# A state-space layer followed by windowed attention: order of the first loads, place of the attention's first loads and of the last statistics

## The chip, the cores and the metric

The kernel runs on one core of one Trainium2 chip. The metric is the device time of one execution in microseconds (us). Before the change it is 6751.26 us, the median of three runs (6746.82 to 6751.3). The profile comes from one more execution, which took 6765.22 us; its first and last instruction are 6763.5 us apart (its span). About 0.2%, or 13.5 us, is what a measurement of this kernel can tell from no change.

## The reference

Input x has shape (4, 384, 64, 64): four batches, 384 channels, 4096 positions each, float32. Two layers follow each other, both with a group normalisation in front and a residual behind:

```
x = x + ssm(gn(x))      # layer norm over channels, in_proj 384 -> 2*768, conv of 4 taps, silu,
                        # x_proj to dt (24), B (16), C (16), softplus, then per position
                        #   h = exp(dt*A)*h + dt*x*B ;  y = sum_n h*C     (16 states per channel)
                        # y + D*x, times silu(z), out_proj 768 -> 384
x = x + attn(gn(x))     # q, k, v = 1x1 conv; 12 heads of 32 channels; each position attends to the
                        # 7x7 window around it (edge padded) with a relative bias; softmax; 1x1 conv
```

The group normalisation takes mean and variance over 32 groups of 12 channels and all 4096 positions of a batch. So the second layer of a batch can't begin before the first layer of that batch has ended.

## The kernel before, in words

**Two layers, written out by hand.** `state_space_layer` works through 44 chunks of 372 or 376 positions, eleven per batch. Each part of a chunk (a load, a matrix product, a scan, a store) is put into a list with a tick; the list is sorted by tick and each engine gets its instructions in that order. `Written` (its `call` is line 152, which is why nearly every row of the profile says L152) ties each instruction of an engine to the one before it, so an engine never takes a later one first. This holds for SP too: SP issues all DMAs of the kernel, in the written order, and one that has to wait holds up all behind it. There are eight completion semaphores for DMAs, used in turn, so that a DMA also waits until the one issued eight before it has landed.

**The start.** Ahead of chunk 0, in a pool `fold` (lines 360 to 426): load `w_in`, `lnw`, `lnb`; load all of batch 0 into `xall` in eight pieces; load `cvb`, `dtb`, `dsk`, `w_cv`, `nega`, `xpw` and six pieces of `w_dt`; multiply `w_in` by `lnb` (PE) for `binp`, scale it by `lnw` (DVE); take the statistics of `xall` (24 `bn_stats`), and turn them into scale and shift `gm` by `stats_phases` (line 256: eight small steps that go PE, DVE, PE, DVE and POOL, PE, ACT, PE, DVE and POOL); store the scaled `w_in` to `wdr` in twelve pieces; build `dcv`, 24 diagonal matrices 128x128 from the identity and `w_cv`, on DVE, and store them to `ddr` in six pieces (lines 420 to 426). Line 469 then loads `qkb` and `pjb`. The first entry of the sorted list is `load_x` of chunk 0 (line 494, tick -732), which loads the tile `xn`; `gn` on ACT normalises it with `gm`, and the layer norm, `in_proj`, `conv` and so on follow.

**The end of the first layer.** Behind the last scan come the last `out_proj`, `residual` (line 799: DVE adds, SP stores to `x1`), and `out_stats` (line 807: `bn_stats` and `bn_aggr` on DVE), for three blocks of channels; then the eight steps of `stats_phases` for the last batch. Values, keys and queries of the second layer for batches 0 to 2 have by then been computed beside the scans and stored to `vdr`, `kdr`, `qdr`.

**The second layer.** `attention_layer` (line 1118) works through 32 stripes of 512 positions with twelve units each, and a loop variable `s` that counts units and starts three stripes early. Its tiles are in pools that open when those of the first layer close, so that the first instruction that writes such a tile waits for the last user of the memory below it. Ahead of unit 0, SP loads `bias` (two pieces, line 1447), `q` and `kt` for stripe 0, the same for stripe 1 (`load_keys`, line 1207), `w_pj`, and the values `vw` of the first pairs (`load_v`, line 1395). `surround` (line 1221) copies edges of `kt` on POOL. A unit has `scores` (PE products into `lg`, DVE adds the bias into `sg` and takes the maximum, ACT exponentiates), `divide` (DVE reciprocal, POOL multiply), `turn` (PE transposes, DVE and ACT copy) one to two units later, and `weigh` (PE) three later. At `s == 4` stands `output_bias`, 18 small products on PE.

Of the kernel before, what the change touches and what calls it, by code (L numbers as in the profile page):

```python
# [25 lines left out]
KC = 4  # L26
# [142 lines left out]
def two_layers(  # L169
# [151 lines left out]
    def store_values(dq, b, k, v):  # L321

        for row in range(2):
# [7 lines left out]
            for t in to:  # L331
                dq.dma_start(vdr[b][t, PAD : PAD + HW, :], v[a : a + HW, :])
                for c, p in ((0, a), (PAD + HW, a + HW - 1)):
# [2 lines left out]
                        v[p : p + 1, :].unsqueeze(1).broadcast_to([1, PAD, C]),  # L336
                    )

    def state_space_layer(eng):
        te, ve, se, ge, _ = eng  # L340
        gm1 = [const.tile([P, NJ, 3], F32, name=f"gm1_{b}") for b in range(NB)]
# [3 lines left out]
        with ExitStack() as es:  # L345
            def pool(name, **kw):
                return es.enter_context(tc.tile_pool(name=name, **kw))
# [13 lines left out]
            with tc.tile_pool(name="fold", bufs=1, side="right") as fold, tc.tile_pool(  # L361
                name="ps_fold", bufs=1, space=PSUM
            ) as fps:
                w_in = load([P, NJ, 2 * DI], in_wT.rearrange("(k p) m -> p k m", p=P), "w_in", fold)
                lnw, lnb = columns((ln_w, NJ, "lnw"), (ln_b, NJ, "lnb"))
                xall = fold.tile([P, NJ, L], F32, name="xall")
                xsrc = x[0].rearrange("(k p) t -> p k t", p=P)
                for k in range(NXT):
                    dq.dma_start(
                        xall[:, :, k * TX : (k + 1) * TX], xsrc[:, :, k * TX : (k + 1) * TX]  # L370
                    )
                cvb, dtb, dsk = columns(
                    (conv_b, ND, "cvb"), (dt_b, ND, "dtb"), (d_skip, ND, "dsk")
                )
                w_cv = load([P, ND, KC], conv_w.rearrange("(k p) m -> p k m", p=P), "w_cv", wt)
                nega = load([P, ND, NS], a_log.rearrange("(k p) n -> p k n", p=P), "nega", wt)
                xpw = load([P, ND, NX], xp_wT.rearrange("(k p) m -> p k m", p=P), "xpw", fold)
                for k in range(3):
                    for half in range(2):
                        d = 3 * half + k  # L380
                        dq.dma_start(
                            w_dt[32 * k : 32 * k + DTR, half * P : (half + 1) * P],
                            dt_wT[:, d * P : (d + 1) * P],
                        )

                se.preload_act_table_set("natural_log_exp_and_others")
                se.activation(nega, nega, AF.Exp)
                se.activation(nega, nega, AF.Copy, scale=-1.0)

                ge.memset(w_xp, 0.0)  # L390
                for k in range(3):
                    ge.tensor_copy(w_xp[:, :, 32 * k : 32 * k + DTR], xpw[:, :, :DTR])
                ge.tensor_copy(w_xp[:, :, 96:], xpw[:, :, DTR:])
                pb0 = fps.tile([P, 512], F32, name="pb0")
                for m in range(2 * ND):
                    for j in range(NJ):
                        te.matmul(
                            pb0[:, m : m + 1], w_in[:, j, m * P : (m + 1) * P], lnb[:, j : j + 1],
                            start=(j == 0), stop=(j == NJ - 1),
                        )  # L400
# [12 lines left out]
                gm0 = small.tile([P, NJ, 3], F32, tag="gm", name="gm_0")  # L413
                for phase in stats_phases(
                    (te, ve, se.activation, ge, lambda t: None), mv0, gm0, lambda: pb0, "a0"
                ):
                    phase()
                for m in range(2 * ND):
                    dq.dma_start(wdr[m], w_in[:, :, m * P : (m + 1) * P])
                dcv = fold.tile([P, ND, KC, P], F32, name="dcv")  # L420
                for d in range(ND):
                    for k in range(KC):
                        ve.tensor_scalar(
                            dcv[:, d, k, :], ident, w_cv[:, d, k : k + 1], None, ALU.mult
                        )
                    dq.dma_start(ddr[d], dcv[:, d, :, :])

            ps_a = pool("ps_a", bufs=1, space=PSUM, reuse_waits="tile")
            ps_x = pool("ps_x", bufs=1, space=PSUM, reuse_waits="tile")
            ps_y = pool("ps_y", bufs=1, space=PSUM, reuse_waits="tile")  # L430
            ps_m = pool("ps_m", bufs=1, space=PSUM, reuse_waits="tile")
            sb = pool("sb", bufs=1, reuse_waits="tile")

            free, kind_of = {}, {}

            def tile_of(shape, tag, bufs, home=sb):

                if tag not in free:
                    free[tag] = [
                        home.tile(shape, F32, name=f"{tag}{k}") for k in range(bufs)  # L440
                    ]
                    for t in free[tag]:
                        kind_of[id(t)] = tag
                return free[tag].pop(0)
# [20 lines left out]

            def put(tick, fn, *args):
                score.append((tick, len(score), fn, args))

            qkb, pjb = columns((qkv_b, 3 * NJ, "qkb"), (proj_b, NJ, "pjb"))


            def x_stats(b, j, i):
# [566 lines left out]
            for b in range(1, NB):  # L1039
# [9 lines left out]
                    put(tick - 3 * STEP, begin)  # L1049
                    put(tick, lambda cell=cell: cell.pop()())  # L1050
                in_phases(T0 - 3 * CHUNK + AT["x_norm"][0], AT["x_norm"][1:], lambda b=b: x_norm(b))
            for b in range(NB):
                in_phases(
                    CHUNK * NCHUNK * (b + 1) + AT["out_norm"][0], AT["out_norm"][1:],
                    lambda b=b: stats_phases(
# [45 lines left out]
                            put(CHUNK * X + AT[name][NJ * i + m], fn, cell, m)  # L1101


            put(-120, dq.dma_start, w_out, out_wT.rearrange("(k p) m -> p k m", p=P))
            put(-120, dq.dma_start, w_v, qkv_wT[:, 2 * C :].rearrange("(k p) m -> p k m", p=P))
            put(-100, lambda: se.activation(qs, qkb[:, 0:NJ], AF.Copy, scale=HD**-0.5))
# [7 lines left out]

            for _, _, fn, args in sorted(score, key=lambda e: e[:2]):
                fn(*args)
        return gm1, qkb, pjb
    def attention_layer(eng, gm1, qkb, pjb):
        te, ve, se, ge, dq = eng
        scale = HD**-0.5  # L1120
        stripes = NB * NXT
        with ExitStack() as es:
# [3 lines left out]
            wt = pool("wt1", bufs=1)  # L1126
            w_qkv = wt.tile([P, NJ, 3 * C], F32, name="w_qkv")
            pjv = wt.tile([P, NJ], F32, name="pjv")
            bias = wt.tile([P, NH, NK], F32, name="bias")
            w_pj = wt.tile([P, NJ, C], F32, name="w_pj")  # L1130

            psum = pool("psum1", bufs=1, space=PSUM)
# [8 lines left out]
            def ring(shape, tag, bufs, k):  # L1141

                if tag not in rings:
                    rings[tag] = [sb.tile(shape, F32, name=f"{tag}{i}") for i in range(bufs)]
                return rings[tag][k % bufs]

            def of(s):
# [57 lines left out]
                surround(s, m)  # L1205

            def load_keys(s):
                b, r = of(s)
                dq.dma_start(
                    q_of(s),  # L1210
                    qdr[b][:, r * TX : (r + 1) * TX].rearrange("(k p) t -> p k t", p=P),
                )
                for m in range(NJ):
                    dq.dma_start(
                        kt_of(s)[:, m, PAD : PAD + RB, PAD : PAD + HW],
                        kdr[b][m * P : (m + 1) * P, r * TX : (r + 1) * TX].rearrange(
                            "p (r c) -> p r c", r=RB
                        ),
                    )

            def surround(s, m):

# [169 lines left out]
                    ov[:, : NJ * P].rearrange("p (m q) -> p m q", m=NJ),  # L1392
                )

            def load_v(k):
                s, p = k // NPAIR, k % NPAIR
                b, r = of(s)
                vw = vw_of(k)
                for e in range(2):
                    for c in range(NCH):  # L1400
                        y, x0 = RB * r + c * RW // NCH, (2 * p + e) * CB
                        dq.dma_start(
                            vw[:KN, e, c, :],
                            vdr[b][y : y + RW // NCH, x0 : x0 + CW, :],
                        )


            N = stripes * UNITS
            waiting = []
            for s in range(-3 * UNITS, N + 12):  # L1410
                stripe, k = s // UNITS, s % UNITS
                for f in waiting:
# [1 line left out]
                waiting = []  # L1414
                if s == 4:
                    output_bias(mm)
                if 0 <= s - 4 < N and (s - 4) % NJ == NJ - 1:
                    keep(s - 4)
                if 0 <= s - 1 < N:
# [24 lines left out]
                        surround(stripe + 2, (k - 4) // 2)  # L1444
                if k == 2 and 0 <= stripe + 3 < stripes and not has_keys(stripe + 3):
                    load_x(stripe + 3)
                if s == 2 - 3 * UNITS:
                    for e in range(2):
                        dq.dma_start(
                            bias[e * QB : (e + 1) * QB].rearrange("p h k -> p (h k)"), bm  # L1450
                        )
                if s == 3 - UNITS:
                    dq.dma_start(w_pj, proj_wT.rearrange("(k p) m -> p k m", p=P))
                if s == 2 * UNITS:
# [2 lines left out]
                    gn(stripe + 3, k - 6)  # L1457
                pair = (s + 1) // NJ + 1
                if (s + 1) % NJ == 0 and 0 <= pair < stripes * NPAIR:
                    load_v(pair)  # L1460

    engines = [
        Written(tc, e) for e in (nc.tensor, nc.vector, nc.scalar, nc.gpsimd, nc.sync)
# [49 lines left out]
```

## Time and profile before

| | us |
|---|---|
| median of three runs | 6751.26 |
| profiled execution | 6765.22 |
| its span | 6763.5 |
| PE, DVE, ACT, POOL busy | 6286.7, 5867.9, 5708.1, 5668.5 |
| last matrix product of the first layer ends | 5246.7 |
| first score of the second layer on DVE | 5271.30 |

An engine's busy time is the sum over its instructions; four engines are busy for 84 to 93% of the span, and waits are spread over both layers. A time line row has the start in us, the duration in us, engine, line, operation and tiles, a count xN where equal ones were merged, and in brackets the idle time before it and what ended it. SPq rows are DMA issues: their duration is that of the issue on SP's queue, not of the transfer. A row of the chain of waits has a start, a duration and what the chain ran through; "issue" is time in which the engine waited for nothing that the profile shows.

### The profile page before, as it was taken

To read this page: it belongs to the slowest core of one execution; us is meant where nothing else is said; L and a number is where in the kernel's file an instruction comes from. 1 tells how busy PE (TensorE), PEld (TensorE's weight loads), DVE (VectorE), ACT (ScalarE), POOL (GpSimd) and SP (SyncE) were. 2 spreads that over 40 slices of the span, in tenths; PEclk is the share of its full clock that TensorE was granted. 3 is DMA by queue.
4 is the path that set the end of the run, shared out by engine and by line. 5 is a ranking of instruction groups with operands and counts; after the bars stand their busy time and mean duration, and the time that the engine had idled before them with its cause. 6 is when DMAs were issued, how large, how long until landed. Compare 5 with 4: busy or idle time off the path is not lost.

```text
span 6763.5 us, 135265 instructions
## 1 busy us (share of the span) xinstructions
PE 6286.7 (93%) x47526; PEld 4326.7 (64%) x47526; DVE 5867.9 (87%) x10258; ACT 5708.1 (84%) x14235; POOL 5668.5 (84%) x2788
## 2 busy tenths in 40 slices
PE   6888888988999999999999999999997899999999
PEld 4666666666667676666666666767665555555555
DVE  3999999999999999999999999999998566555555
ACT  3888888888999999999999999999996687665556
POOL 1999999999999999999999999999999555443443
PEclk9999999999999999999999999999998899999999
DMA  5242423233454535354444434453532555323332
GB/s 179 83 136 87 138 86 118 91 116 115 135 159 127 160 117 166 119 158 133 153 140 131 153 121 151 123 160 117 160 113 67 169 156 152 103 95 104 102 102 91
DMA packets 790241, 860.11 MB, mean 127 GB/s; under 512 B 200345, under 2 KB 710073, under 8 KB 789433
## 3 DMA queue, kind: packets, MB, share of 16 engines
q1 hardware_dynamic: 789560, 851.45, 40.7%
q8 instruction: 377, 6.18, 0.4%
q14 instruction: 304, 2.48, 0.1%
HBM read 740.60 MB, written 110.81 MB: 126 GB/s over the span
## 4 chain that ended last, share of the span: by engine, by line
PE 43%; ACT 21%; DVE 20%; issue 6%; POOL 6%; DMA 3%; SPq 1%; POOLq 0%; DVEq 0%; ACTq 0%
PE mm L152 28%; DVE h L152 17%; PE yps L152 7%; ACT da L152 6%; POOL h L152 6%; PE pt L152 4%; ACT L152 4%; ACT sg L152 3%; PE ov L152 2%; PE lg L152 2%; DMA w_in<-wdr 2%; ACT dt L152 1%; ACT sz L152 1%; ACT xb L152 1%; ACT pT L152 1%
## 5 line engine op out<-in xcount | busy, mean ns | idle before, releaser
L152 DVE TENSOR_TENSOR_SCAN h<-da,h 128x373 f32<-128x373 f32 (+1 forms) x4224 | 3658.6, 914 | 124.8 <-ACT da L152 109.7
L152 POOL TENSOR_TENSOR h<-h,BC 128x1488 f32<-128x1488 f32 (+1 forms) x1056 | 3255.9, 3100 | 116.6 <-ACT state L152 110.7
L152 ACT ACTIVATE da<-dt,nega 128x372 f32<-128x372 f32 (+1 forms) x4224 | 2361.7, 569 | 212.0 <-DVE h L152 194.3
L152 POOL TENSOR_TENSOR h<-dtx,BC 128x372 f32<-128x372 f32 (+5 forms) x836 | 1757.9, 2113 | 51.7 <-ACT dtx L152 41.2
L152 PE MATMUL yps<-ident,h 128*124 128x128 f32 (+1 forms) x12672 | 1587.2, 279 | 104.8 <-POOL h L152 104.5
L152 PEld LDWEIGHTS yps<-ident,h 128*124 128x124 f32 (+1 forms) x12672 | 1453.5, 142 | 261.2 <-POOL h L152 165.8
L152 PE MATMUL mm<-xn,w_in 128*128 128x372 f32 (+3 forms) x3168 | 1146.5, 503 | 102.4 <-DMA w_in<-wdr 47.7
L152 POOL TENSOR_TENSOR sg<-sg,rs 128x784 f32<-128x784 f32 x384 | 573.4, 1493 | 635.5 <-DVE rs L152 507.4
L152 ACT ACTIVATE sg<-sg,mx 128x196 f32<-128x196 f32 x1536 | 685.3, 448 | 389.8 <-DVE mx L152 381.2
L152 DVE TENSOR_TENSOR h<-dtxps,BC 128x1488 f32<-128x1488 f32 (+5 forms) x924 | 964.5, 1059 | 6.5 <-ACT dtx L152 4.6
L152 PEld LDWEIGHTS mm<-xn,w_in 128*128 128x128 f32 x3168 | 603.7, 200 | 470.5 <-issue 49.5
L152 PE MATMUL mm<-xb,cw 128*128 128x372 f32 (+1 forms) x2112 | 697.8, 476 | 7.1 <-DMA cw<-ddr 5.1
L152 ACT ACT_TABLE_LOAD x529 | 678.7, 1283 | 10.1 <-PEq L1498 0.8
L152 DVE CUSTOM_DVE_ANT_0 sg<-lg,bias 128x196 f32<-128x196 f32 x1536 | 464.4, 358 | 196.7 <-PE lg L152 195.6
L152 PE MATMUL mm<-yg,w_out 128*128 128x372 f32 (+1 forms) x1584 | 529.5, 480 | 22.0 <-DVE yg L152 21.9
L152 PEld LDWEIGHTS mm<-xb,cw 128*128 128x128 f32 x2112 | 389.8, 189 | 239.2 <-DVE h L152 6.0
L152 PE MATMUL pt<-ident,sg 128*98 128x128 f32 x3072 | 447.6, 281 | 29.5 <-ACT pT L152 21.3
L152 PEld LDWEIGHTS pt<-ident,sg 128*98 128x98 f32 x3072 | 314.4, 128 | 182.4 <-issue 81.6
L152 PEld LDWEIGHTS mm<-yg,w_out 128*128 128x128 f32 x1584 | 290.0, 190 | 183.7 <-DVE yg L152 30.3
L152 PEld LDWEIGHTS ov<-pT,vw 98*32 98x32 f32 x12288 | 189.8, 110 | 195.5 <-issue 139.5
L152 PE MATMUL mm<-xk,wk 128*128 128x256 f32 x1080 | 268.3, 390 | 46.2 <-ACT dt L152 46.2
L152 ACT ACTIVATION_READ_ACCUMULATOR sg<-sg,mx 128x1 f32 x1536 | 288.2, 188 | 0.0
(136 smaller groups left out, 7158.9 us busy)
## 6 DMA issues: line engine op xcount, KB each, us to landing
BC<-bcrows SPq DMA_DIRECT2D x320, 744.0 KB
w_in<-wdr SPq DMA_DIRECT2D x528, 192.0 KB
vw<-vdr SPq DMA_DIRECT2D x512, 147.0 KB
cw<-ddr SPq DMA_DIRECT2D x264, 256.0 KB
xs<-in_x_dram SPq DMA_DIRECT2D x210, 186.0 KB
wk<-in_qkv_wT_dram SPq DMA_DIRECT2D x180, 192.0 KB
o<-x SPq DMA_DIRECT2D x96, 256.0 KB
out_dram<-o SPq DMA_DIRECT2D x96, 256.0 KB
```

Source lines behind the costliest of these rows:

```text
L152: ins = made(*args, **kw)
```

## The change

The arithmetic stays the same. Three things are moved.

At the start, `w_cv` is loaded ahead of `xall`; `qkb` and `pjb` are loaded with the other small vectors; `dcv` is built on POOL instead of DVE, and its six stores stand ahead of the statistics and of the twelve stores of `wdr`:

```diff
                 lnw, lnb = columns((ln_w, NJ, "lnw"), (ln_b, NJ, "lnb"))
+                w_cv = load([P, ND, KC], conv_w.rearrange("(k p) m -> p k m", p=P), "w_cv", wt)
                 xall = fold.tile([P, NJ, L], F32, name="xall")
...
+                cvb, dtb, dsk, qkb, pjb = columns(
+                    (conv_b, ND, "cvb"), (dt_b, ND, "dtb"), (d_skip, ND, "dsk"),
+                    (qkv_b, 3 * NJ, "qkb"), (proj_b, NJ, "pjb"),
+                )
...
+                dcv = fold.tile([P, ND, KC, P], F32, name="dcv")
+                for d in range(ND):
+                    for k in range(KC):
+                        ge.tensor_scalar(
+                            dcv[:, d, k, :], ident, w_cv[:, d, k : k + 1], None, ALU.mult
+                        )
+                    dq.dma_start(ddr[d], dcv[:, d, :, :])
                 se.preload_act_table_set("natural_log_exp_and_others")
...
                 for m in range(2 * ND):
                     dq.dma_start(wdr[m], w_in[:, :, m * P : (m + 1) * P])
-                dcv = fold.tile([P, ND, KC, P], F32, name="dcv")
-                for d in range(ND):
-                    for k in range(KC):
-                        ve.tensor_scalar(
-                            dcv[:, d, k, :], ident, w_cv[:, d, k : k + 1], None, ALU.mult
-                        )
-                    dq.dma_start(ddr[d], dcv[:, d, :, :])
```

At the end of the first layer, the tiles that are not needed by its last instructions (`xn`, `sq`, `w_in`, `xb`, `cw`, `xd`, `xk`, `yk`, `wk`, `xv`, `vo`) now have a pool `prep` of their own on the right side of the memory. It closes behind the last of their users, and in its place opens a pool `early` with `kt` for stripes 0 and 1, `q` for stripe 0, `vw` for pair 0 and `bias`. Their loads are put at a tick behind the first `residual` of the last chunk and ahead of its second (605), so in SP's order the stores of the second and third `residual` stand behind them. `load_keys` and `load_v` leave out what is there:

```diff
+            def begin_attention():
+                preps.close()
+                home = ctx.enter_context(
+                    tc.tile_pool(name="early", bufs=1, reuse_waits="tile", side="right")
+                )
...
+                for s in range(2):
+                    load_stripe_keys(dq, kt[s], s)
+                load_stripe_queries(dq, q, 0)
+                load_pair_values(dq, vw, 0)
+                for e in range(2):
+                    dq.dma_start(bias[e * QB : (e + 1) * QB].rearrange("p h k -> p (h k)"), bm)
+
+            put(
+                CHUNK * (len(chunks) - 1) + 1 + max(
+                    max(AT[name]) for name in ("key_store", "value_store", "in_bias", "conv")
+                ),
+                begin_attention,
+            )
...
             def load_keys(s):
...
+                if s > 0:
+                    load_stripe_queries(dq, q_of(s), s)
+                if s > 1:
+                    load_stripe_keys(dq, kt_of(s), s)
...
                 if (s + 1) % NJ == 0 and 0 <= pair < stripes * NPAIR:
-                    load_v(pair)
+                    if pair > 0:
+                        load_pair_values(dq, vw_of(pair), pair)
```

The eight steps of `stats_phases` for the last batch leave the end of the first layer. One of them is taken in each unit from `s` = 5 to 12, with the product bank `mm` of the second layer:

```diff
-            for b in range(NB):
+            for b in range(NB - 1):
                 in_phases(
...
+            last_stats = stats_phases(
+                (te, ve, se.activation, ge, lambda t: None), mv, gm1[NB - 1], lambda: mm, "b3"
+            )
             for s in range(-3 * UNITS, N + 12):
...
                 if s == 4:
                     output_bias(mm)
+                if s > 4 and last_stats:
+                    last_stats.pop(0)()
```

More of the change, by code (lines that the diff above doesn't have):

```diff
@@ L337, in store_values, with load_stripe_keys, load_stripe_queries, load_pair_values @@
                     )
+    def load_stripe_keys(dq, kt, s):
+        b, r = s // NXT, s % NXT
+        for m in range(NJ):
+            dq.dma_start(
+                kt[:, m, PAD : PAD + RB, PAD : PAD + HW],
+                kdr[b][m * P : (m + 1) * P, r * TX : (r + 1) * TX].rearrange(
+                    "p (r c) -> p r c", r=RB
+                ),
+            )
+    def load_stripe_queries(dq, q, s):
+        b, r = s // NXT, s % NXT
+        dq.dma_start(
+            q, qdr[b][:, r * TX : (r + 1) * TX].rearrange("(k p) t -> p k t", p=P)
+        )
+    def load_pair_values(dq, vw, k):
+        s, p = k // NPAIR, k % NPAIR
+        b, r = s // NXT, s % NXT
+        for e in range(2):
+            for c in range(NCH):
+                y, x0 = RB * r + c * RW // NCH, (2 * p + e) * CB
+                dq.dma_start(vw[:KN, e, c, :], vdr[b][y : y + RW // NCH, x0 : x0 + CW, :])
     def state_space_layer(eng):
@@ L371, in state_space_layer @@
                     )
-                cvb, dtb, dsk = columns(
-                    (conv_b, ND, "cvb"), (dt_b, ND, "dtb"), (d_skip, ND, "dsk")
+                cvb, dtb, dsk, qkb, pjb = columns(
+                    (conv_b, ND, "cvb"), (dt_b, ND, "dtb"), (d_skip, ND, "dsk"),
+                    (qkv_b, 3 * NJ, "qkb"), (proj_b, NJ, "pjb"),
                 )
-                w_cv = load([P, ND, KC], conv_w.rearrange("(k p) m -> p k m", p=P), "w_cv", wt)
                 nega = load([P, ND, NS], a_log.rearrange("(k p) n -> p k n", p=P), "nega", wt)
@@ L432, in state_space_layer, with tile_of @@
             sb = pool("sb", bufs=1, reuse_waits="tile")
+            preps = ExitStack()
+            prep = preps.enter_context(
+                tc.tile_pool(name="prep", bufs=1, reuse_waits="tile", side="right")
+            )
+            short = {"xn", "sq", "w_in", "xb", "cw", "xd", "xk", "yk", "wk", "xv", "vo"}
             free, kind_of = {}, {}
-            def tile_of(shape, tag, bufs, home=sb):
+            def tile_of(shape, tag, bufs, home=None):
+                home = home or (prep if tag in short else sb)
                 if tag not in free:
@@ L467, in put @@
                 score.append((tick, len(score), fn, args))
-            qkb, pjb = columns((qkv_b, 3 * NJ, "qkb"), (proj_b, NJ, "pjb"))
             def x_stats(b, j, i):
@@ L1101, in state_space_layer @@
                             put(CHUNK * X + AT[name][NJ * i + m], fn, cell, m)
+            early = {}
+            def begin_attention():
[3 more added lines that the diff above has]
+                )
+                kt = early["kt"] = [
+                    home.tile([P, NJ, RW, HP], F32, name=f"kt{s}") for s in range(2)
+                ]
+                q = home.tile([P, NJ, TX], F32, name="q0")
+                vw = home.tile([P, 2, NCH, C], F32, name="vw0")
+                bias = early["bias"] = home.tile([P, NH, NK], F32, name="bias")
+                early["q"], early["vw"] = [q], [vw]
+                for s in range(2):
+                    load_stripe_keys(dq, kt[s], s)
+                load_stripe_queries(dq, q, 0)
+                load_pair_values(dq, vw, 0)
+                for e in range(2):
+                    dq.dma_start(bias[e * QB : (e + 1) * QB].rearrange("p h k -> p (h k)"), bm)
+            put(
+                CHUNK * (len(chunks) - 1) + 1 + max(
+                    max(AT[name]) for name in ("key_store", "value_store", "in_bias", "conv")
+                ),
+                begin_attention,
+            )
             put(-120, dq.dma_start, w_out, out_wT.rearrange("(k p) m -> p k m", p=P))
@@ L1116, in state_space_layer, with attention_layer @@
                 fn(*args)
-        return gm1, qkb, pjb
-    def attention_layer(eng, gm1, qkb, pjb):
+        return gm1, qkb, pjb, early, mv1[NB - 1]
+    def attention_layer(eng, gm1, qkb, pjb, early, mv):
         te, ve, se, ge, dq = eng
@@ L1128, in attention_layer @@
             pjv = wt.tile([P, NJ], F32, name="pjv")
-            bias = wt.tile([P, NH, NK], F32, name="bias")
+            bias = early["bias"]
             w_pj = wt.tile([P, NJ, C], F32, name="w_pj")
@@ L1143, in ring @@
                 if tag not in rings:
-                    rings[tag] = [sb.tile(shape, F32, name=f"{tag}{i}") for i in range(bufs)]
+                    rings[tag] = list(early.get(tag, ()))
+                    for i in range(len(rings[tag]), bufs):
+                        rings[tag].append(sb.tile(shape, F32, name=f"{tag}{i}"))
                 return rings[tag][k % bufs]
@@ L1207, in load_keys @@
             def load_keys(s):
[L1208 to L1219, printed above, removed]
+                if s > 0:
+                    load_stripe_queries(dq, q_of(s), s)
+                if s > 1:
+                    load_stripe_keys(dq, kt_of(s), s)
             def surround(s, m):
@@ L1393, in keep @@
                 )
[L1395 to L1405, printed above, removed]
             N = stripes * UNITS
             waiting = []
+            last_stats = stats_phases(
+                (te, ve, se.activation, ge, lambda t: None), mv, gm1[NB - 1], lambda: mm, "b3"
+            )
             for s in range(-3 * UNITS, N + 12):
@@ L1446, in attention_layer @@
                     load_x(stripe + 3)
[L1447 to L1451, printed above, removed]
                 if s == 3 - UNITS:
```

## Prediction

> **What bounds the kernel now.** I read the page first: PE 93%, DVE 87%, ACT 84%, POOL 84% busy, and a chain that ended last made of PE 43%, ACT 21%, DVE 20%, "issue" 6%, DMA 3%. In the long middle the four engines hand work round with little air; the change touches none of that. What it touches are two places where all engines stand still: the first 62 us, and the seam between the layers near 5250 us. I therefore took the chain of waits in these two stretches, then SP's time line, since SP issues every DMA in written order.
>
> The chain of waits at the start:
>
> ```profile
> 28.77 14.25 DVE stx L152 x24
> ...
> 49.65 4.80 DVE dcv L152 x24
> ...
> 56.12 4.97 DMA xn<-in_x_dram
> ...
> 61.17 1.29 ACT xn L152 x2
> ```
>
> SP's time line there:
>
> ```profile
> 27.71 2.54 SPq L152 DMA_DIRECT2D w_dt<-in_dt_wT_dram  x6
> 30.36 8.17 SPq L152 DMA_DIRECT2D wdr<-w_in  x12
> 50.55 4.24 SPq L152 DMA_DIRECT2D ddr<-dcv  x6
> 54.84 0.45 SPq L152 DMA_DIRECT2D qkb<-in_qkv_b_dram  x1
> 55.34 0.73 SPq L152 DMA_DIRECT2D pjb<-in_proj_b_dram  x1
> 56.12 0.49 SPq L152 DMA_DIRECT2D xn<-in_x_dram  x1
> ```
>
> See the hole between 38.5 and 50.5: SP stands at the first store of `dcv`, which DVE makes only after the statistics (last step of `gm`: POOL, 49.78 + 0.20 = 49.98). The request for chunk 0's `xn` is behind it. So ACT could start at 50.0 and starts at 61.17: **11.2 us** in which nothing but a badly queued DMA is awaited.
>
> The seam. First SP's time line, then the first score on DVE, then the windows (span; busy us of PE, PEld, DVE, ACT, POOL; PE clock; DMA share; GB/s):
>
> ```profile
> 5240.11 0.38 SPq L152 DMA_DIRECT2D xs<-in_x_dram  x1
> 5243.48 4.12 SPq L152 DMA_DIRECT2D x<-xs  x2
> 5250.18 1.17 SPq L152 DMA_DIRECT2D bias<-bm  x2
> 5251.40 0.57 SPq L152 DMA_DIRECT2D q<-qdr  x1
> 5252.02 8.52 SPq L152 DMA_DIRECT2D kt<-kdr  x3
> 5260.57 1.07 SPq L152 DMA_DIRECT2D q<-qdr  x1
> 5261.69 5.77 SPq L152 DMA_DIRECT2D kt<-kdr  x3
> ```
>
> ```profile
> 5271.30 0.36 DVE L152 CUSTOM_DVE_ANT_0 sg<-lg,bias 128x196 f32<-128x196 f32 x1 [15.56 <-PE lg L152]
> ```
>
> ```profile
> 5250.00:5260.00 10.00, 3.61 (x20) 3.27 (x20) 0.47 (x3) 0.45 (x2) 0.78 (x4) 0.50 0.86 200
> 5260.00:5270.00 10.00, 0.00 (x0) 0.00 (x0) 0.00 (x0) 0.00 (x0) 3.57 (x15) 0.50 1.15 241
> 5290.00:5300.00 10.00, 9.35 (x225) 6.04 (x224) 7.65 (x41) 9.82 (x39) 7.85 (x12) 1.00 0.31 94
> ```
>
> The loads wait for the last `bn_aggr` (ends 5249.98), then take until 5269.25 to the first keys of stripe 1: 19 us in which the DMA engines are the only busy part. The small statistics chain (5248 to 5256) lies wholly beside them and costs nothing today.
>
> **The start, step by step.** The queue up to `w_dt` is paced by `xall` landing; `w_cv` only trades its place with `qkb`, and `pjb` adds its 0.73. So `w_dt` ends near 30.25 + 0.75 = 31.0. Six stores of `ddr` follow. Their `dcv` is now POOL's: no row shows that operation at this size; near rows are POOL's TENSOR_SCALAR 128x512 at 768 ns (a quarter is 192) and its COPY 128x144 at 306 ns, so 24 x 0.19 to 0.31 = 4.6 to 7.3 us; I take 7. POOL is free from 4.2 us; `w_cv` is asked for right behind `lnb`, which landed at 10.14, so POOL is through by about 19, with 12 us of cover before SP comes; each operation would have to take 0.8 us before it showed. What was queued behind on POOL, the `w_xp` copies (1.09 us, waiting for `xpw` until 30.46), isn't late. Stores: 6 x 0.32 (their shortest issue) to 0.7 = 1.9 to 4.2, then `wdr` 8.17, so SP reaches `xn` at 41.5 to 43.5. The built program adds one wait there: `xn` now lies over `xall` and waits for the last `bn_stats`, 43.0; behind it in SP's queue stand only the first `w_in` and `cw`, wanted at in_proj, 14.4 us after `gn`. From 43.2, with today's 4.97 us to land, `xn` is there at 48.2, before `gm` at 49.98. If the 3.9 MB of stores go only at the 240 GB/s measured in 30 to 40 us, they end at 31 + 16.4 = 47.4 and `xn` lands near 52. So `gn` starts at 50.1 to 52: gain 9 to 11.1, I take **11.0**. DVE loses 4.80 us of `dcv`, which nobody but SP waited for. What follows, `gn` to the first scan, hangs on `gn` and moves as a block; next late is `gm` itself.
>
> **The seam, step by step.** In SP's order the early loads stand right behind the load of `xs` at 5240.11 + 0.38, so they start at 5240.5 instead of 5250.2. The memory they land in has long been free. But two things are not as good as they look. First, what must land is about as much: keys 6 x 256 KB, q 768, values 4 x 147, bias 2 x 588 = 4.17 MB (before: bias, two q, keys = 4.35). Second, **a new wait**: the stores of the second and third `residual` are now behind all these loads on SP, and `sg`, which DVE's first score writes, lies in a pool that opens only when every user of the old one is through, these stores included (the built program shows both waits). POOL's copy of keys into stripe 2's tile waits for them too, with the remaining copies of stripe 1 and the first `divide` behind it. So the first score needs 4.17 + 0.39 = 4.55 MB moved from 5240.5.
>
> How long is that? The row: before, 3.82 MB were landed at 5269.25, 19.1 us after 5250.18, 200 GB/s with all latencies (241 in the best window). Piece by piece from steady rows (5309.71 to 5319: q and three keys 6.1 us, four values 3.2) I get 2 x 5.7 for keys, 2.4 for q, 3.2 for values, 6 for bias, 1 for stores = 24, and by the same prices 22 for the old list against 19 to 20.5 seen; scaled, 21 to 22. At 200 GB/s: 22.8; at 241: 18.9. I take 21.8: DVE's first score at **5262.3**, against 5271.30, gain **9.0** (6 to 12). The rule: the Trainium skill, "DMA: Bandwidth & Descriptors", Specifications and the anatomy of one DMA, gives a core's share of HBM as about 358 GB/s and a fixed cost near 2 us. By that estimate 4.55 MB need 14.7 us, the score starts at 5255.2 and the gain is 16. The trace has never moved this mix that fast (keys go in 256-byte pieces), so I go by the row and keep the rule's value for the low end.
>
> The next loads keep their distance: `w_pj` and the next values were issued 3.8 us before to 3.7 after the first score, and will be 0.5 to 5 after it; `output_bias` wants `w_pj` 9.8 us after it (5281.1). Keys of stripe 2 are asked for about 1.3 us later relative to it; POOL's idle gaps of 0.4 to 3.5 us per unit cover that.
>
> A rule that speaks against hoping for more: the same skill's "TensorE: Matmul & The Clock Gate" says that an idle window of about 3.4 us halves PE's clock. The trace has 0.50 from 5250 to 5280. PE will still idle from 5246.7 to the keys (about 5256) and again to 5262, so the units after it start at half clock as before: 0. By the rule alone (3.4 us at half) a closed gap would have given 1.7, by the trace (seven units in 18.5 us where 7 x 2.43 = 17.0) 1.5.
>
> **The deferred statistics** get dearer. They were covered by the loads; now they stand in PE's queue between units, with PE 9.35 and ACT 9.82 of 10 us busy. Their products at full clock, from the same four steps at the start: 0.64 + 1.41 + 0.48 + 1.44 = 3.97 us; ACT 0.45, DVE 0.5, POOL 0.8 beside them. The row for what such an insertion costs is `output_bias`: 2.17 us of PE, and that unit took 5.2 us instead of 2.45. Against this, PE has about 0.15 us free per unit, 1.2 over eight. Between 2 and 5; I take **3.7**. Their result is wanted only some twenty stripes later.
>
> **Sum** for the profiled execution: 6765.2 - 11.0 - 9.0 + 3.7 = 6748.9, a gain of 16.3 us, 0.24%. The executions without the profile had the median 6751.26; the gain is one of stalls and carries over: **6735.0**. Own range: 12 to 20 us, 6731 to 6739.
>
> **Rivals.** (1) The loads vanish: bulk moves at the rule's rate and the stores slip through, so the first score follows the last `bn_aggr` at about 5251. For: SP has ten idle microseconds, the share was 0.22 in 5240 to 5250. Against: 4.55 MB would need 430 GB/s. 11 + 20 - 3.7 = 27.3: 6724. (2) The wait on loads is only replaced by the wait on the stores: keys issue as slowly as before (8.52 + 5.77 us), bias and stores queue behind, and the score starts near 5269; or `xn` lands late. For: `kt` issues of up to 4.96 us[...]. 11 + 2 - 3.7 = 9.3: 6742, within what can't be told from no change. (3) Slower: splitting the pool moves nearly every tile of the 44 chunks to another address. For: 4224 scans of 914 ns and 1056 POOL products of 3100 ns give small effects a long lever. Against: nothing in the trace shows time by address. It decides from 16.3/4224 = 3.9 ns per scan (0.4%); at 0.8% the kernel would lose 33 - 16 = 17 us: 6768. (4) The start does nothing, because `xn` waits for something else of the old pool: gain 5.3, 6746; its only new wait ends at 43.0, which speaks against it.
>
> **Numbers.** Forecast 0.66, (1) 0.12, (2) 0.14, (3) 0.05, (4) 0.03. The range leaves out (3), (4) and the ends of (1): 6721 to 6744. Faster by over 0.2% (13.5 us, about what a measurement tells from no change): most of the forecast and (1), 0.72; same: 0.23; slower: 0.05.
>
> **What would show it.** In the changed profile: `ddr` stores ahead of `wdr` with no hole in SP's line, `xn` issued near 43, `gn` near 50; `kt` issued from about 5229.5 (5240.5 less 11), the two `x` stores behind `bias`; the first score on DVE about 20 us earlier than 5271.3 and ended by a DMA, not by PE; four units between `s` = 5 and 12 longer by about a microsecond. If the first score follows `bn_aggr` at once, (1) holds; if scans or POOL products have other means, (3).

## The result, and the profile after

| | before | changed |
|---|---|---|
| median of 11 runs each, us | 6751.3 (6746.82 to 6757.78) | 6734.49 (6726.21 to 6740.87) |
| ratio of the two, with its 95% interval | | 0.9975 (0.9966 to 0.9984) |
| profiled execution, us | 6765.22 | 6732.91 |
| its span, us | 6763.5 | 6731.2 |

The changed kernel is 0.25% faster, 16.8 us by the medians; the interval of the ratio allows 11 to 23.

**The start.** SP's time line of the changed kernel:

```profile
28.37 2.54 SPq L152 DMA_DIRECT2D w_dt<-in_dt_wT_dram  x6
31.03 3.10 SPq L152 DMA_DIRECT2D ddr<-dcv  x6
34.22 8.23 SPq L152 DMA_DIRECT2D wdr<-w_in  x12
42.82 0.39 SPq L152 DMA_DIRECT2D xn<-in_x_dram  x1
```

The hole of twelve microseconds in front of the `ddr` stores is gone; the queue runs through to `xn`. ACT's first row of `gn`, and the last step of the statistics on POOL that it now waits for:

```profile
49.77 1.87 ACT L152 ACTIVATE xn<-xn,gm 128x372 f32<-128x372 f32 x3 [2.06 <-POOL zero L152]
```

```profile
49.55 0.19 POOL L152 TENSOR_TENSOR gm<-gm 128x3 f32<-128x3 f32 x1 [2.94 <-DVE gm L152]
49.68 0.10 POOL L152 MEMSET zero<- 128x4 f32 x1
```

`gn` starts at 49.77 instead of 61.17, and what ends its wait is the statistics, no longer a DMA.

**The seam.** SP's time line, then the first scores on PE, then the first on DVE:

```profile
5218.43 0.38 SPq L152 DMA_DIRECT2D xs<-in_x_dram  x1
5218.90 5.92 SPq L152 DMA_DIRECT2D kt<-kdr  x6
5224.86 1.14 SPq L152 DMA_DIRECT2D q<-qdr  x1
5226.05 3.13 SPq L152 DMA_DIRECT2D vw<-vdr  x4
5229.28 1.14 SPq L152 DMA_DIRECT2D bias<-bm  x2
5230.52 1.38 SPq L152 DMA_DIRECT2D x<-xs  x2
```

```profile
5231.04 0.96 PE L152 MATMUL lg<-kt,q 32*64 32x196 f32 x16 [6.07 <-DMA q<-qdr]
5243.65 1.29 PE L152 MATMUL lg<-kt,q 32*64 32x196 f32 x16 [11.65 <-POOL kt L152]
```

```profile
5242.75 0.36 DVE L152 CUSTOM_DVE_ANT_0 sg<-lg,bias 128x196 f32<-128x196 f32 x1 [14.45 <-DMA x<-xs]
```

Keys and queries were there for PE at 5231.04. DVE could not take the scores until 5242.75, when the residual stores had landed (`x<-xs`: SBUF tile `xs` to the DRAM tensor printed as `x`). They stand behind all of the early loads. The semaphore updates kept in the trace tell when a transfer had landed (sixteen updates for each of these): the second half of the bias at 5241.62, the last store at 5242.29. So the store ended the wait by only 0.7 us, and the bias would have ended it otherwise. POOL's key copies into stripe 2's tile waited for the same store, and PE's second group of scores for these copies. So the wait of the old seam (keys) has been exchanged for a shorter one (bytes of the early loads, then the stores).

The chain of waits from 5230 on, start and duration, says the same:

```profile
5230.52 0.53 SPq L152
5231.05 0.06 issue
5231.16 11.13 DMA x<-xs
5242.44 0.08 issue
5242.52 0.67 POOL kt L152 x3
```

**Where the time went.** Absolute starts drift by several microseconds from one execution to the next, so I cut each profiled execution at four marks: the start of `gn` on ACT; the third `residual` of the last chunk on DVE; the first score on DVE; the 17th `divide` reciprocal on DVE (that stretch holds `output_bias` and the deferred statistics).

| us | before | changed |
|---|---|---|
| start of `gn` | 61.17 | 49.77 |
| `gn` to third residual ("loop") | 5185.52 | 5175.24 |
| third residual to first score ("seam") | 24.61 | 17.74 |
| first score to 17th reciprocal ("first units") | 45.93 | 47.15 |
| from there to the end | 1446.3 | 1441.3 |

What the change touched gives 11.4 + 6.9 - 1.2 = 17.1 us, and the medians say 16.8. The profiled executions differ by 32.3; the remaining 15 lie in the loop and in the rest of attention. Before's profiled execution was 14 us slower than its median, the changed kernel's 1.6 us faster, and that is the surplus. Such drift is seen in the experiments below too: those two stretches took 5169 to 5181 and 1441 to 1446 over nine other kernels, among them two with the old placement of the tiles (5170.06 and 5176.93). So I don't count the 15 us as an effect of the change.

### The profile page after: what moved, and what is told of

It is laid out like the page before. It is cut to its first block, busy times and chain, and to the rows that moved or that the text cites. A ratio compares the mean times of both kernels' runs of the same rounds, so it can differ in the third digit from the quotient of the medians.

```text
span 6731.2 us, 135270 instructions
## 1 busy us (share of the span) xinstructions
PE 6266.0 (93%) x47526; PEld 4311.4 (64%) x47526; DVE 5860.2 (87%) x10234; ACT 5707.5 (85%) x14235; POOL 5682.5 (84%) x2812
## 4 chain that ended last, share of the span: by engine, by line
PE 42%; ACT 20%; DVE 20%; POOL 8%; issue 7%; DMA 3%; SPq 1%; POOLq 0%; DVEq 0%; ACTq 0%
PE mm L152 27%; DVE h L152 17%; POOL h L152 7%; PE yps L152 7%; ACT da L152 6%; PE pt L152 4%; ACT L152 3%; ACT sg L152 3%; PE ov L152 2%; DMA w_in<-wdr 2%; PE lg L152 2%; ACT dt L152 1%; ACT pT L152 1%; ACT sz L152 1%; ACT xb L152 1%
## 5 line engine op out<-in xcount | busy, mean ns | idle before, releaser
L152 PEld LDWEIGHTS mm<-yg,w_out 128*128 128x128 f32 x1584 | 291.3, 191 | 185.3 <-DVE yg L152 30.9
```

What stands on the lines that cost most here:

```text
L152: ins = made(*args, **kw)
```

## The experiments

The marks of all kernels; "ended by" is what released DVE's first score. In 1 and 7 the row names a load, but the score starts 1.2 us after the start of PE's first products, just as in 3 and 9, so it is these that it waited for. Each ratio below is to runs of the kernel before that stood beside that experiment (medians 6752.94 for 1 to 4, 6753.63 for 5 to 7, 6754.94 for 8 and 9, against 6751.3 for the changed kernel), so medians of different rows are comparable to a few us only.

| | `gn` | loop | seam | first units | first score ended by |
|---|---|---|---|---|---|
| changed | 49.77 | 5175.24 | 17.74 | 47.15 | store of `x` |
| 1 start alone | 49.83 | 5176.93 | 23.75 | 46.12 | PE's scores |
| 2 `dcv` on DVE | 49.91 | 5177.71 | 18.07 | 47.08 | store of `x` |
| 3 deferral alone | 60.65 | 5170.06 | 23.68 | 48.51 | PE's scores |
| 4 no deferral | 49.72 | 5172.57 | 18.55 | 46.13 | store of `x` |
| 5 stores on ACT | 50.04 | 5169.31 | 21.03 | 47.16 | load of `bias` (see there) |
| 6 loads earlier | 49.60 | 5175.59 | 3.63 | 48.55 | last `bn_aggr` |
| 7 loads earlier, no deferral | 49.66 | 5180.75 | 14.31 | 45.96 | PE's scores |
| 8 bias earlier | 49.68 | 5178.45 | 10.47 | 47.11 | store of `x` |
| 9 stores on ACT, bias first | 50.33 | 5180.31 | 14.70 | 47.10 | PE's scores |

My theory: the start is worth its queue hole; the seam is set by the bytes that must land between the first early load and the first score; the deferral costs a little. The rival for the seam: it is the order (the stores that stand behind the loads), not the bytes.

**1. The start alone.** Before, with only the first part of the change (`w_cv` early, `dcv` on POOL, `ddr` stores ahead of the `wdr` stores).

```diff
+                w_cv = load([P, ND, KC], conv_w.rearrange("(k p) m -> p k m", p=P), "w_cv", wt)
                 xall = fold.tile([P, NJ, L], F32, name="xall")
...
+                        ge.tensor_scalar(
+                            dcv[:, d, k, :], ident, w_cv[:, d, k : k + 1], None, ALU.mult
+                        )
+                    dq.dma_start(ddr[d], dcv[:, d, :, :])
```

> The kernel before with the start part alone. Theory (the store of dcv, made behind the statistics, held up the request for xn on SP's queue; the three parts of the change add up): gn starts at 49.8 us instead of 61.2 as in the whole change, the seam from the start of the third residual to the first score stays at 24.6 us, and the total is 11 us (0.16%) below the kernel before, two thirds of the gain of 16.8. Rival (the head start is eaten by the main loop, whose pace something else sets): gn at 49.8, but the total within 3 us of before.

Median of 21 runs 6746.88, ratio 0.9989 (0.9982 to 0.9995), a gain of 3 to 12 us. `gn` starts at 49.83, 11.3 us earlier, and the seam is within a microsecond of before. The 11.3 are near the upper end of what the runs allow (the medians differ by 6.1), and the rival's 3 lies just outside. That the head start is there is shown; that all of it reaches the end is not.

**2. `dcv` back on DVE, at its new place.**

```diff
-                        ge.tensor_scalar(
+                        ve.tensor_scalar(
```

> The changed kernel with dcv built by DVE at its new, early place instead of by POOL. Theory (the place in the queues counts, not the engine): DVE is idle until 25.6 us, builds the 24 matrices from about 10.2 in 24 x 0.28 = 6.7 us, and gn starts at 49.8 as in the changed kernel. Rival (taking the work off DVE is what gained): the statistics and gn come 5 to 7 us later, near 55 to 57.

`gn` starts at 49.91, and the one run took 6735.28 us, so the rival's 5 to 7 us are not there. DVE was through with `dcv` at 15.1 us, long before its statistics. The engine doesn't matter; that the work and its stores stand ahead of the statistics does.

**3. The deferral alone.** Before, with only the last batch's statistics taken in units 5 to 12.

```diff
-            for b in range(NB):
+            for b in range(NB - 1):
...
+                if s > 4 and last_stats:
+                    last_stats.pop(0)()
```

> The kernel before with only the last batch's statistics deferred into units 5 to 12. Theory (in the old kernel the statistics lay beside the loads, so deferring gains nothing and adds its own price): seam 24.6 us as before; the time from the first score to the 17th divide 1.2 us longer than before's 45.9, as in the changed kernel; total +1 us, which no timing can tell from 0. Rival (my blind price): +3.7 us over these units. Rival (the statistics held up the seam): seam shorter by up to 5.8 us.

Ratio 1.0002 (0.9994 to 1.001): no gain, no loss that can be told. The seam stays within a microsecond of before (23.68 against 24.61), so the statistics had not held it up. The first units take 2.6 us more, which neither the theory (1.2) nor the rival (3.7) had said; the part on the prediction comes back to it.

**4. The changed kernel without the deferral.**

```diff
-            for b in range(NB - 1):
+            for b in range(NB):
...
-                if s > 4 and last_stats:
-                    last_stats.pop(0)()
```

> The changed kernel with the last batch's statistics back at the end of the first layer. Theory (the seam is set by the loads and the stores behind them, 14.5 us of DVE idle, so 5.8 us of statistics fit beneath): seam 17.7 us as in the changed kernel, first score to 17th divide 45.9 instead of 47.1, total 1 us below the changed kernel, not to be told from it. Rival (the deferral earns its place): the seam grows by up to 5.8 us and the total by 3 to 5.

Median 6733.85, ratio 0.9971 (0.996 to 0.9983), beside 6734.49 of the changed kernel. The seam is 0.8 longer, the first units 1.0 shorter. In this change the deferral is neutral, as expected: the loads would have hidden the statistics, and the units nearly do.

**5. The last two residual stores on ACT's queue**, so that they no longer stand behind the early loads. This is the test of order against bytes.

```diff
-                dq.dma_start(x1s[b][m * P : (m + 1) * P, t0 : t0 + T], xr)
+                own = se if X == len(chunks) - 1 and m > 0 else dq
+                own.dma_start(x1s[b][m * P : (m + 1) * P, t0 : t0 + T], xr)
```

> The changed kernel with the stores of the last chunk's second and third residual issued from ACT's queue, so that they no longer stand behind the early loads on SP. Theory A (the amount that has to land sets the seam: bias is the last early load and the score needs it): the first score is ended by a DMA of bias, and the seam shrinks by only 0.5 to 2 us from 17.7. Theory B (the stores behind the loads set it: their place in the queue, not bias): the seam shrinks by 4 us or more.

Both theories missed: the seam grew to 21.03 (median 6741.45, ratio 0.9982 (0.9974 to 0.999)). POOL's and DVE's rows of this kernel:

```profile
5223.84 2.42 POOL L152 COPY kt<-kt 128x210 f32<-128x210 f32 x9 [2.14 <-DMA x<-xs]
```

```profile
5240.38 0.36 DVE L152 CUSTOM_DVE_ANT_0 sg<-lg,bias 128x196 f32<-128x196 f32 x1 [17.73 <-DMA w_pj<-in_proj_wT_dram]
```

The stores were down by 5223.84, but the first score came 16.5 us later, with other DMAs still landing. In the changed kernel SP stands until the stores have landed and issues the next `q` only then, at 5242.42. Here nothing stopped it, and it issued the next `q`, `w_pj` and `vw` right behind the bias, from 5225.16 on:

```profile
5223.84 1.14 SPq L152 DMA_DIRECT2D bias<-bm  x2
5225.16 0.46 SPq L152 DMA_DIRECT2D q<-qdr  x1
5226.23 0.41 SPq L152 DMA_DIRECT2D w_pj<-in_proj_wT_dram  x1
5226.81 9.33 SPq L152 DMA_DIRECT2D vw<-vdr  x4
```

It was the bias, last of the early loads and now sharing the DMA engines with these, that was missing: its second half landed at 5239.85, half a microsecond before the score. `w_pj`, which the row names and the score doesn't read, had only half of its updates by then (the last at 5242.96). Experiment 9 puts the bias first.

**6. The early loads a hundred ticks earlier**, ahead of the last chunk's first `out_proj` instead of behind its first `residual`.

```diff
-                CHUNK * (len(chunks) - 1) + 1 + max(
-                    max(AT[name]) for name in ("key_store", "value_store", "in_bias", "conv")
-                ),
+                CHUNK * (len(chunks) - 1) + 492,
                 begin_attention,
```

> The changed kernel with the early loads at tick 492 of the last chunk instead of 597, ahead of the first residual's store. Both theories of the seam say that 4.6 MB behind the last residual are what is waited for; SP is idle for 35 us before that. So: kt is issued about 35 us before the third residual instead of 6 us before it, everything has landed when out_proj ends, the first score follows the last bn_aggr (3.4 us after the start of the third residual, against 17.7), PE's clock no longer falls to 0.5 there, and the total is 14 to 16 us below the changed kernel, about 6719. Rival (something else was next late, such as the release of the old pool by the last store, or kt's copies on POOL): seam of 8 us or more.

**Median 6720.33 (6715.12 to 6735.34), ratio 0.9955 (0.9942 to 0.9967)**: faster than both kernels, 14.2 us under the median of the changed one, and the seam is 14.1 shorter. SP's and DVE's rows:

```profile
5183.78 5.54 SPq L152 DMA_DIRECT2D kt<-kdr  x6
...
5193.74 1.14 SPq L152 DMA_DIRECT2D bias<-bm  x2
```

```profile
5228.03 0.45 DVE L152 BATCH_NORM_AGGREGATE mv<-st 128x2 f32<-128x66 f32 x1
5228.82 0.36 DVE L152 CUSTOM_DVE_ANT_0 sg<-lg,bias 128x196 f32<-128x196 f32 x1 [0.34 <-DVE mv L152]
```

The loads now run beside the last scans, the stores find the DMA engines nearly free (busy share 0.14 from 5224 to 5230), and the score follows the last `bn_aggr` at once. One part of the expectation failed: PE's clock still fell to 0.50, and the first units took 1.4 us more than in the changed kernel. That is rival (1) of the prediction, reached by the place of the loads and not by their rate.

**7. The same without the deferral.** The edits of 6 and 4 together:

```diff
-            for b in range(NB - 1):
+            for b in range(NB):
...
+                CHUNK * (len(chunks) - 1) + 492,
                 begin_attention,
...
-                if s > 4 and last_stats:
-                    last_stats.pop(0)()
```

> The kernel with loads at tick 492 and the last batch's statistics back at the end of the first layer. Theory (deferral pays only once nothing else covers the statistics): the seam is 9 us (3.4 + 5.8), 5.8 longer than with deferral, the units after it 1.2 us shorter, so 4 to 5 us slower than with deferral. Rival (deferral never pays, since the steps run beside the first scores): no difference in the seam.

Median 6729.72, ratio 0.9963 (0.995 to 0.9977); the seam is 14.31, 10.7 more than in 6. The statistics are no longer covered, and POOL, whose steps of them are in its queue, comes to the key copies only behind them:

```profile
5239.50 0.20 POOL L152 TENSOR_TENSOR gm<-gm 128x3 f32<-128x3 f32 x1 [2.82 <-DVE gm L152]
5239.64 6.22 POOL L152 COPY kt<-kt 128x24 f32<-128x24 f32 x24
```

```profile
5243.55 0.96 PE L152 MATMUL lg<-kt,q 32*64 32x196 f32 x16 [4.32 <-POOL kt L152]
```

PE's first scores wait for these copies until 5243.55. The expectation, a seam of 9 and a loss of 4 to 5 us, had left the copies out. Against them stand 2.6 us in the first units, so by the trace the deferral is worth about 8 us here (9.4 by the medians), and nothing where loads hide the statistics.

**8. The bias alone at the earlier tick.** 1.2 MB less between the first of the other loads and the score, with the stores still behind all of them. Bytes and order, which the times of 5 had not told apart, say different things here.

```diff
+            def begin_rest():
+                for s in range(2):
+                    load_stripe_keys(dq, early["kt"][s], s)
+                load_stripe_queries(dq, early["q"][0], 0)
+                load_pair_values(dq, early["vw"][0], 0)
...
+            put(
+                CHUNK * (len(chunks) - 1) + 492,
+                begin_attention,
+            )
...
-                begin_attention,
+                begin_rest,
```

> The given change with the bias alone (1.2 MB) loaded at tick 492, ahead of the first out_proj of the last chunk, the other early loads staying at tick 597. Theory A (the amount of bytes between the first early load and the first score ends the wait): 1.2 MB less at about 200 GB/s are 6 us, so the seam (third residual to first score on DVE) falls from 17.7 to 11.7, within 1.5, and the first score is still ended by a DMA. Theory B (the order ends it: the x loads of stripe 2 wait for the residual stores that stand behind all early loads, whatever their bytes): the seam falls by no more than the issue time of the two bias pieces, 1.2 us, to 16.5. Time by A about 6 us below the given change's 6734.5, so about 6728; by B within 2 us of it.

The seam is 10.47, 7.3 shorter; median 6728.99, ratio 0.9962 (0.9949 to 0.9976). DVE's first score:

```profile
5238.60 0.36 DVE L152 CUSTOM_DVE_ANT_0 sg<-lg,bias 128x196 f32<-128x196 f32 x1 [7.17 <-DMA x<-xs]
```

The releaser is still the store, with the same order around it, and it comes by the bytes earlier: 1.2 MB in 7.3 us are 165 GB/s. So the store only marks the end of the queue of bytes before it. Theory A holds (11.7, within 1.5, was expected); B (order alone) had allowed 1.2 us.

**9. Stores on ACT's queue and the bias first of the early loads.**

```diff
             def begin_attention():
...
+                for e in range(2):
+                    dq.dma_start(bias[e * QB : (e + 1) * QB].rearrange("p h k -> p (h k)"), bm)
                 for s in range(2):
                     load_stripe_keys(dq, kt[s], s)
                 load_stripe_queries(dq, q, 0)
                 load_pair_values(dq, vw, 0)
```

> The kernel with the last two residual stores on ACT's queue, with the bias as the first of the early loads instead of the last. Theory A (in that kernel the bias, last in the order of the loads that the first score needs, ended its wait, as the bytes were shared with the loads issued behind it): now keys, queries or their products end it; the keys land later by the bias's share, so the seam is 18 to 21 and the first score is ended by PE or by DMA of keys, no better than the given change's 17.7 by more than 1. Theory B (w_pj or some other load outside the early list ended it): the first score stays ended by a DMA at 21, within 1. Theory C (only the bias was late, keys long there): the seam falls to about 12.

Seam 14.70: 6.3 less than in 5, so neither `w_pj` nor any load behind the early list had ended the wait there (B falls), and the bias had. But keys and queries were not long there either (C falls), and A's floor of 18 was too high. PE's and DVE's rows:

```profile
5244.18 0.96 PE L152 MATMUL lg<-kt,q 32*64 32x196 f32 x16 [13.59 <-DMA q<-qdr]
```

```profile
5245.34 0.36 DVE L152 CUSTOM_DVE_ANT_0 sg<-lg,bias 128x196 f32<-128x196 f32 x1 [11.41 <-PE lg L152]
```

Now `q`, the last thing needed, ends it. The landing times by the semaphore updates, in us from the start of the third residual, say the same for all four kernels: the score follows whichever of the three comes last, within 0.4 to 0.6 us, or 1.3 where PE's products stand between:

| | `q` | bias | last store | first score |
|---|---|---|---|---|
| changed | 5.8 | 16.6 | 17.3 | 17.7 |
| 5 stores on ACT | 6.9 | 20.5 | 4.2 | 21.0 |
| 8 bias earlier | 6.2 | long before | 10.0 | 10.5 |
| 9 stores on ACT, bias first | 13.4 | 3.0 | 5.8 | 14.7 |

Median 6731.52, ratio 0.9966 (0.9954 to 0.9979). Its seam is 3.0 shorter than the changed kernel's; the interval of its ratio overlaps that kernel's.

## Why the prediction was right

The forecast of 6735.0 met 6734.49, and the case that was called likeliest is what the trace shows. Its terms:

| us | predicted | measured |
|---|---|---|
| start | 11.0 | 11.4 |
| seam | 9.0 | 6.9 |
| deferral | -3.7 | -1.2 |
| sum | 16.3 | 17.1 (medians: 16.8) |

**The start** was right step by step: `w_dt` through at 30.9 (31.0 predicted), `xn` issued at 42.82 (43.2 predicted), `gm` next late, as said. That all of the head start would reach the end was taken for granted; experiment 1 leaves that open (6.1 us by its medians, 3 to 12 by its interval). One term was mis-sized. `dcv` on POOL took 13.91 us where I took 7 from near rows by size:

```profile
10.22 13.91 POOL L152 TENSOR_SCALAR dcv<-ident,w_cv 128x128 f32<-128x128 f32 x24 [6.74 <-DMA w_cv<-in_conv_w_dram]
24.07 0.74 POOL L152 MEMSET w_xp<- 128x768 f32 x1
```

It cost nothing, because the bound (0.8 us each before it shows) was above the 0.58 that each took. The cover was worth working out; the estimate alone would not have been safe.

**The seam** had the right mechanism, the new wait on the stores included, and a size too good. The loads started 6.1 us before the third residual (6.2 predicted). From there to the first score the 4.55 MB took 23.85 us, 191 GB/s, not 21.8. The step that failed is the scaling "24 by pieces, scaled down to 21 to 22 because the old list came out faster than its pieces": unscaled, it would have been right, though for the old list the same prices had been too high. What the prediction had no term for shows in the windows of the changed kernel (same columns as in the prediction):

```profile
5218.00:5230.00 12.00, 6.97 (x23) 3.85 (x21) 3.74 (x8) 0.00 (x0) 3.76 (x15) 0.92 1.05 233
5230.00:5242.00 12.00, 0.96 (x16) 0.36 (x16) 0.00 (x0) 0.00 (x0) 0.00 (x0) 0.50 0.81 178
```

In the second half the DMA engines are no longer all busy. The semaphore updates of the last store come in two groups, nine by 5239.49 and seven from 5241.72 to 5242.29, and those of both halves of the bias are split in the same way. Each of the four loads of `vw` ahead of them has one update just behind its issue and ends in seven. Before, where `vw` came behind the bias, all sixteen updates of a half of the bias came within 1.0 us. This fits seven of the sixteen engines carrying the values and being late with all that stands behind. If the remaining bytes had been spread evenly, the store would have landed near 5240.7, an estimate from the two groups (nine sixteenths at 5239.49, seven at 5242.29): 1.6 of the 2.1 us that the seam was missed by. No run here changed the shape of `vw`, so this is argued, not shown.

The Trainium skill's figure, about 358 GB/s for a core ("DMA: Bandwidth & Descriptors", Specifications), would have given 14.7 with the fixed 2 us, which the page's section on the anatomy of one DMA states for DMAs that GpSimd issues, and 12.7 without. The same section wants 512 bytes or more per piece for full rate, and the DMA view of the changed kernel between 5218 and 5243 shows what the mix is made of:

```profile
DMA packets 7796, 4.94 MB, mean 197 GB/s; under 512 B 6380, under 2 KB 7284, under 8 KB 7668
...
q1 hardware_dynamic: 7796, 4.94, 89.0%
```

The engines were 89% busy at 197 GB/s, and four packets in five are under 512 bytes. The measurement and the condition agree; no run here changed the size of the pieces, so that it is the cause is not shown.

**The deferral** cost a third of what was taken. The four products on PE took 0.48, 0.82, 0.33 and 0.82 = 2.45 us, not 3.97:

```profile
5257.62 0.48 PE L152 MATMUL mm<-mv,grp 128*32 128x1 f32 x6
...
5263.06 0.82 PE L152 MATMUL mm<-gmean_b,grpT 32*128 32x1 f32 x6
...
5268.38 0.33 PE L152 MATMUL mm<-dev_b,grp 128*32 128x1 f32 x6
...
5273.55 0.82 PE L152 MATMUL mm<-grs_b,grpT 32*128 32x1 f32 x6
```

This is the mis-sized term: the durations came from the steps at the start, where the six products of a `grpT` step lie 0.21 us apart on a PE that is otherwise idle; between units they lie 0.11 apart. The clock was 1.00 in both places, so it isn't the clock; what it is stays open. With the 1.2 us that the prediction counted as free on PE, 2.45 leaves 1.25, which is what showed: the first units grew by 1.0 to 1.2 in the changed kernel. In experiments 3 and 6 they grew by 2.6. There the granted clock, from 16 to 20 us behind the first score, was still 0.50; in the changed kernel it was 0.98, and in the remaining kernels 0.83 or more. The added 1.4 us lie in the two units from about 18.6 us on. Why the clock came back later in these two is open.

The two errors, a seam that gained 2.1 less and a deferral that cost 2.5 less, cancelled: the total was met by luck more closely than its terms deserve.

**The rivals.** (1) is not what this change does, but experiment 6 gets there. (2) has its mechanism in the trace (the stores end the wait), at a seam of 17.7 instead of 22 or more. (3) falls: the scans 128x373 take 913 ns each in both kernels, POOL's products 128x1488 take 3096 ns before and 3095 now, and over the kernels with the new placement the loop took 5169 to 5181, against 5170.06, 5176.93 and 5185.52 in the three with the old one. (4) falls with `gn` at 49.77. That PE's clock would stay low was right: 0.50 from 5230 to 5242.

## What to carry to other kernels

When loads are put earlier, count what must land before the first consumer, stores behind them included, against the rate that this mix of pieces has had in the trace; moving them under work that leaves the DMA engines free (here a hundred ticks) gained more than reordering them. Ask of a moved piece of work what covers it at the old place and at the new one, and ask again when that cover goes: the same deferral was worth nothing here and about 8 us once the loads were hidden. A releaser named by a wait may be only the last of a queue; take bytes away without changing the order, and see whether it moves, or look up when each transfer landed.

## What the runs showed of the hardware

**A small operation on POOL is not a quarter of one four times as long.** Two groups of POOL in the changed kernel (count, then busy us and mean ns):

```profile
L152 POOL TENSOR_SCALAR xp<-xp,gm 128x512 f32<-128x512 f32 x51 | 39.2, 768 | 0.0
...
L152 POOL TENSOR_SCALAR dcv<-ident,w_cv 128x128 f32<-128x128 f32 x24 | 13.9, 602 | 6.7 <-DMA w_cv<-in_conv_w_dram 6.7
```

A quarter of the elements takes 78% of the time, although the larger operation multiplies and adds and the smaller one only multiplies. DVE did the same 24 in 4.80 us before, 0.20 each.

**PE's clock came back slowly.** In experiment 6 PE was idle for 3.38 us ahead of 5229.83 and then busy again. Its windows (span; busy us of PE, PEld, DVE, ACT, POOL; PE clock; DMA share; GB/s):

```profile
5230.00:5234.00 4.00, 3.34 (x36) 2.15 (x37) 1.80 (x15) 3.00 (x15) 2.77 (x7) 0.50 0.91 302
5234.00:5238.00 4.00, 4.00 (x34) 2.64 (x36) 3.39 (x17) 3.77 (x16) 2.76 (x2) 0.50 0.96 273
5238.00:5242.00 4.00, 4.00 (x71) 3.52 (x71) 0.46 (x3) 0.91 (x3) 0.49 (x1) 0.87 1.03 236
5242.00:5246.00 4.00, 4.00 (x67) 3.10 (x65) 2.81 (x17) 2.98 (x12) 3.37 (x6) 0.55 0.68 178
5246.00:5250.00 4.00, 4.00 (x64) 2.71 (x66) 2.27 (x14) 3.06 (x12) 2.32 (x6) 0.59 0.29 87
5250.00:5254.00 4.00, 4.00 (x112) 3.03 (x112) 2.72 (x14) 3.19 (x14) 1.77 (x3) 1.00 0.33 119
```

With PE's rows full from 5234 on, the granted clock is at 0.50 for some eight microseconds, comes up to 0.87 for four, falls to 0.55 and 0.59, and is at 1.00 only about twenty after the restart. The other ten traces have the same course: 0.50 for at least the first six microseconds behind the first score, up for a few, 0.50 again, and 1.00 from 16 to 22 on. So an idle stretch of 3.4 us cost these units as many slow microseconds as the 23 us in front of PE's first scores in experiment 3, and closing the seam brought no warm start.
